# First loads in steps, splits moved to a unit's ends, comparisons in two passes and a last unit in eight products, in a gated expert layer with a diffusion step

## The chip, the cores and the metric

The kernel runs on one core of a Trainium2 chip. The metric is the device time of one execution in microseconds; lower is better. A core has TensorE (PE, matrix products into PSUM, with PEld its weight loads), VectorE (DVE), ScalarE (ACT), GpSimd (POOL) and SyncE (SP, which here issues nearly all DMAs). Each engine works through its own instructions in order and waits on semaphores for the others.

## The reference

`x` is 128 sequences of 64 rows of 256. Each sequence has a type; one of five experts is chosen by it, and two shared dense layers run for all. The three outputs are mixed by softmax weights made from row 0 of each, and added to `x`. Then one explicit diffusion step with reflecting edges and a reaction term is added, with three factors per sequence.

```python
def dense(x, wi, wo): return relu(x @ wi) @ wo          # 256 -> 1024 -> 256
s0, s1 = dense(x, swi[0], swo[0]), dense(x, swi[1], swo[1])
eo = relu(x @ wi[type_label]) @ wo[type_label]
w = softmax(relu(concat(eo[:, 0], s0[:, 0], s1[:, 0]) @ g1) @ g2)
y = x + eo * w[0] + s0 * w[1] + s1 * w[2]
lap_x = y[:, :, left] - 2 * y + y[:, :, right]          # reflecting pads
lap_y = y[:, up, :] - 2 * y + y[:, down, :]
out = y + zX * lap_x + zY * lap_y + zR * y * (1 - y)
```

## The kernel before, in words

**Numbers in two parts.** Every matmul operand is split into a high part that the fast f32 format of PE holds and a rest (`split`: ACT writes the high part, DVE or POOL subtracts). A product of two split operands is three matmuls (high by high, high by low, low by high).

**The shared layers.** The rows are cut into 16 tiles of 4 rows for all 128 sequences (512 columns). Two tiles (a and b, index l) and one shared layer make an *item*: items 0 to 15, item n holding pair n // 2 and layer n % 2. An item is four *units* q of 256 hidden columns. `unit` computes the two tiles by two hidden blocks with seven block products in place of eight, from sums of x blocks (T1 to T4) and of weight blocks (S1 to S4, made by `sum_wi`, split by `split_wi`, kept in DRAM by `keep_wi`, loaded again for later pairs by `load_wi`). Its products run in this order: A11 (seeds bank pa, ACT copies it into pb), S2, A12, S3, S1 (bank pd), A22, S4. DVE forms `c` from pd and the copy u; S4 accumulates on pd and so follows the reading of it by c. After A11, A12, S1 and at the end stand the four *hooks* of a unit, numbered 0 to 3, counted through the item as k = 4q + j; `at(k, ...)` puts background work there. Between the products stand the second-layer products of the unit before (`acc`, lines 662 to 692): *wide* ones with the hidden block's high part (512 columns) and *narrow* ones with its low part (256 columns). `hidden` takes the relu on ACT and the rest on DVE.

**Stages.** Items 0 and 1 come first, and while they run the weights of all eight shared units are prepared (`prepare`, `again`, lines 876 to 890) and the sequences are put in an order by expert (`order_batches`, five steps called as `order`). The very first unit pair has its weights before any sums are ready: `plain_units` (line 616) computes units 0 and 1 of item 0 with eight products. Then come the grouped expert products (`stream`), written to DRAM as `eo_d` in groups of sequences. Items 2 to 15 follow; at item 2 the gate's weights are made (`gate_shared`, `gate_expert` and so on). From item 2 on each tile of y is loaded, gets its expert and shared parts (`start_y`, `sums`, `evacuate`) and is diffused (`diffuse_a`, `diffuse_b`) in two halves of two rows; the halo rows of a tile come from its neighbour (`halo`).

**The start.** `load_behind` and the loop above it (lines 191 to 209) issue the loads of x blocks and weight units on SP; a one-column copy on POOL makes a load wait until the first x block has landed.

**The end.** Item 15 goes through `shared_item`, then `end_rows` (line 743): tile 14's diffusion, then for each row of tile 15 the second-layer products, the evacuation, and `begin_row` and `end_row`, which diffuse row by row and store each.

**Order.** From `in_order(True)` on, the program order written in the code is the order of each engine; in `stream` it is off and a scheduler orders DVE, ACT and POOL. Tiles come from pools with a fixed number of buffers: 6 PSUM banks for most products and 2 for pb (`seeded`), 25 buffers of 4 KB and 16 of 2 KB a partition, 2 for the split weights of a unit. A new tile waits for the readers of the buffer that it takes.

Of the kernel before, what the change touches and what calls it, by code (L numbers as in the profile page):

```python
# [16 lines left out]
P = 128  # L17
B, S, D, F = 128, 64, 256, 1024
NE = 5
# [23 lines left out]
def cond_resid_kernel(ctx: ExitStack, tc: tile.TileContext, xg, xs, xn, itok, z, we, ws, g1, g2, out):  # L43
# [147 lines left out]
    def load_behind(u, c0, c1):  # L191
        if u not in wsr:
            wsr[u] = slot4(f"wsr{u}", F32)
        gps.tensor_copy(wsr[u][:, 0, c0 : c0 + 1], xraw[0, 0, 0][:, 0:1])
        load_ws(u, c0, c1)
# [4 lines left out]
    for l in range(2):  # L200
        for k in range(2):
            if l == 1:
                xraw[0, k, l] = slot2(f"xr0_{k}{l}")
                gps.tensor_copy(xraw[0, k, l][:, 0:1], xraw[0, 0, 0][:, 0:1])
                dma(xraw[0, k, l], xs[l, :, k, :])
    load_behind(0, 256, 512)
    load_behind(1, 0, 512)
    load_behind(2, 0, 512)
    load_behind(3, 0, 512)
# [20 lines left out]
    def order_batches():  # L230
# [72 lines left out]
        ge = [const.tile([1, NU], F32, name=f"ge{i}") for i in range(2)]  # L303
        gt = const.tile([1, NU], F32, name="gt")
        vec.tensor_scalar(ge[0], first, base[0:1, 1:2], None, ALU.is_ge)
        vec.tensor_scalar(ge[1], first, base[0:1, NE : NE + 1], float(NE - 1), ALU.is_lt, ALU.mult)
        for e in range(2, NE):
            vec.tensor_scalar(gt, first, base[0:1, e : e + 1], None, ALU.is_ge)
            vec.tensor_add(ge[0], ge[0], gt)
        yield  # L310
        for e in range(NE + 1, 2 * NE):
            vec.tensor_scalar(gt, first, base[0:1, e : e + 1], None, ALU.is_ge)
            vec.tensor_add(ge[1], ge[1], gt)
# [6 lines left out]
    def clear_spare():  # L320

        zero = pool4.tile([P, ST * D], F32, tag="t4", name="zero")
        vec.memset(zero, 0.0)
        r0, r1 = GROUPS[NRUN][0] * NT, NSLOT * NT
        for r in range(r0, r1, P):
            n = min(P, r1 - r)
            dma(eo_d[r : r + n, :], zero[:n, :])
# [161 lines left out]
    def half_rows(t, half):  # L489
        if t == 0:  # L490
            return (2, 2) if half == 0 else (4, 1)
        return (1 + 2 * half, 2)
# [8 lines left out]
    def diffuse_a(t, half, eng=gps, edge=gps):  # L501
# [6 lines left out]
        act.activation(q[:, :n, :], c, AF.Identity, bias=cz[:, 0:1], scale=cz[:, 1:2])  # L508
        edges(a[:, :n, :], c, edge)
        eng.tensor_tensor(a[:, :n, 1 : D - 1], c[:, :, 0 : D - 2], c[:, :, 2:D], ALU.add)  # L510
# [17 lines left out]

    part, zy = {}, {}

    def end_tile(name):
        return small.tile([P, D], F32, tag="s2", name=name)

    def begin_row(r):

        c = yb[NT - 1][:, r, :]
        a, q, zy[r] = (end_tile(f"end_{n}{r}") for n in "aqz")
        last = r == ST + 1
        act.activation(q, c, AF.Identity, bias=cz[:, 0:1], scale=cz[:, 1:2])
        act.activation(zy[r], c, AF.Copy, scale=zt[:, 1:2])  # L540
        vec.tensor_tensor(a[:, 1 : D - 1], c[:, 0 : D - 2], c[:, 2:D], ALU.add)
        edges(a, c, act)
        vec.tensor_mul(q, q, c)
        if last:
            vec.tensor_add(q, q, part[r])
        vec.scalar_tensor_tensor(q, a, zt[:, 0:1], q, ALU.mult, ALU.add)
        if r == ST:
            part[r + 1] = end_tile("end_p")
            act.activation(part[r + 1], c, AF.Copy, scale=cz[:, 2:3])
        part[r] = q  # L550
        if r <= ST:
            vec.tensor_add(q, q, zy[r - 1])

    def end_row(r, queue):
        if r <= ST:
            vec.tensor_add(part[r], part[r], zy[r + 1])
        queue.dma_start(out[:, ST * (NT - 1) + r - 2, :], part[r])

# [56 lines left out]

    def plain_units():
# [4 lines left out]
        def weights(u):  # L621
            w.append(slot4(f"wi_plain{u}").rearrange("p h c -> p (h c)").rearrange("p (h f c) -> p h f c", h=2, f=2))
            split(w[u][:, 0, :, :], w[u][:, 1, :, :], wsr[u][:, :, 0:256], vec)

        def tile(u, l, bank=psum):
            x = (xop[0, B11], xop[0, B21]) if l == 0 else (x12, xop[0, B22])
            ps = [bank(f"pu{u}{l}{f}") for f in range(2)]
            for k in range(2):
                for j, (wp, xp) in enumerate(((0, 0), (0, 1), (1, 0))):
                    for f in range(2):  # L630
                        mm(
                            ps[f], w[u][:, wp, f, k * P : (k + 1) * P], x[k][:, xp, :], k + j == 0, k == 1 and j == 2
                        )
            return [lambda f=f: hidden((ha, hb)[l], (0, 2 * u + f), ps[f]) for f in range(2)]
# [6 lines left out]
        for i in (T1, T2):  # L641
            sum_x(0, i, vec)
        run(tile(0, 0))
        weights(1)
        for i in (T3, T4):
            sum_x(0, i, vec)
        run(tile(0, 1))
        split_wo(0)
        wide, narrow = tile_a(0, 0)
        run(tile(1, 0))  # L650
        sum_wi(2, gps)
# [5 lines left out]
        keep_wi(2)  # L657
        run(tile(1, 1, seeded))
# [49 lines left out]
    def shared_item(n, before, bg):  # L708

        last, first = n == 2 * NP - 1, n == 0  # L710
        for q in range(NQ):
# [9 lines left out]
            if first and q == 0:  # L721
                plain_units()
            elif not first or q > 1:
                unit(n, q, gaps, hooks)
# [345 lines left out]
```

## Time and profile before

| | us |
|---|---|
| median of 3 runs (1069.48 to 1069.96) | 1069.76 |
| the profiled execution | 1069.37 |
| its span, first to last instruction | 1067.3 |
| PE busy in the span | 1045.0 |
| DVE busy | 740.1 |
| ACT busy | 542.5 |
| POOL busy | 228.0 |

The mean granted clock of PE is 0.995. Times in the profile are us from the first instruction. A line of the order of time has the start, the length, the engine, the kernel's line, the operation, the tile written and the tiles read, the shapes and a count; in brackets stands how long the engine was idle before it and what ended that. L97 and L82 are helper lines that record every DVE, ACT and POOL operation and every matmul, so groups are told apart by their tiles. Lengths of matmuls are modelled and overlap; the distance from start to start is the pace.

### The profile page before, as it was taken

Reading aid. Unit: us, or ns where it says so; the run is one execution under the profiler, and the core shown is the slowest. Engines: PE = TensorE matmul, PEld = TensorE weight load, DVE = VectorE, ACT = ScalarE, POOL = GpSimd, SP = SyncE. Lnnn points to the kernel's source line nnn. Section 1 sums busy time; section 2 is a strip of 40 time slices with the busy share of each in tenths; the row PEclk is TensorE's granted clock in tenths of the full one; section 3 lists DMA queues with packets and bytes.
Section 4 is the critical chain, followed back from the end, with each engine's and each line's share of the span. In section 5 each row is a group of like instructions: output and inputs, shape, how many; then the busy total and the mean of one; then the engine's idle time right before and its main releaser. Section 6 shows DMA issues by size and latency. Waiting matters only on the chain.

```text
span 1067.3 us, 15675 instructions
## 1 busy us (share of the span) xinstructions
PE 1045.0 (98%) x5478; PEld 893.9 (84%) x5478; DVE 740.1 (69%) x1289; ACT 542.5 (51%) x1005; POOL 228.0 (21%) x220
## 2 busy tenths in 40 slices
PE   8999999999999999999999999999999999999995
PEld 6878888888888889988878888888888888888885
DVE  6786745455455556857879778687687687686768
ACT  5565645554455546653446445455355364364353
POOL 3212100100001000221252232242242152052020
PEclk9999999999999999999999999999999999999998
DMA  5347454344443465726335344344253254244221
GB/s 173 124 162 252 151 163 151 119 139 159 159 137 119 139 197 181 244 101 222 109 124 186 124 145 163 104 168 159 73 203 129 69 202 154 80 167 163 105 89 45
DMA packets 65601, 156.12 MB, mean 146 GB/s; under 512 B 7568, under 2 KB 33936, under 8 KB 65520
## 3 DMA queue, kind: packets, MB, share of 16 engines
q1 hardware_dynamic: 62896, 146.18, 40.6%
q0 software_dynamic: 2480, 8.78, 2.3%
q8 instruction: 44, 0.72, 0.3%
q14 instruction: 37, 0.30, 0.1%
q10 hardware_dynamic: 144, 0.13, 0.0%
HBM read 130.16 MB, written 24.90 MB: 145 GB/s over the span
## 4 chain that ended last, share of the span: by engine, by line
PE 53%; DVE 3%; ACT 0%; issue 0%; DVEq 0%
PE acc L82 27%; PE pb L82 11%; PE pd L82 7%; PE pa L82 7%; DVE end_q L97 1%; DVE lq L97 1%; DVE yb L97 0%; DVE x L97 0%; PE pgs L82 0%; DVE end_a L97 0%; DVE pd L97 0%; DVE c L97 0%; DVE lb L97 0%; DVE la L97 0%; ACT pb L97 0%
## 5 line engine op out<-in xcount | busy, mean ns | idle before, releaser
L82 PE MATMUL up<-gxh,gw 128*128 128x512 f32 (+1 forms) x608 | 179.6, 362 | 0.0
L82 PE MATMUL pb<-x,wi 128*128 128x512 f32 x558 | 159.5, 394 | 2.2 <-ACT u L97 1.9
L82 PE MATMUL gacc<-gw,gh 128*128 128x512 f32 (+1 forms) x608 | 141.7, 375 | 0.0
L97 DVE SCALAR_TENSOR_TENSOR gl<-up,gh 128x512 fp32r<-128x512 f32 x112 | 77.0, 688 | 90.1 <-ACT gh L97 90.0
L97 ACT ACTIVATE gh<-up 128x512 fp32r<-128x512 f32 (+1 forms) x152 | 81.8, 539 | 110.4 <-PE up L82 109.5
L97 DVE TENSOR_TENSOR gw<-gwr,gw 128x512 fp32r<-128x512 f32 x152 | 105.4, 722 | 43.9 <-ACT gw L97 43.5
L82 PEld LDWEIGHTS gacc<-gw,gh 128*128 128x128 f32 x608 | 110.0, 188 | 20.9
L82 PEld LDWEIGHTS up<-gxh,gw 128*128 128x128 f32 x608 | 110.5, 189 | 16.5
L97 ACT ACTIVATE u<-pb 128x512 f32<-128x512 f32 x124 | 74.2, 598 | 93.7 <-PE pb L82 89.1
L82 PEld LDWEIGHTS pb<-x,wi 128*128 128x128 f32 x558 | 99.4, 189 | 21.4 <-ACT u L97 3.6
L97 ACT ACTIVATE gw<-gwr 128x512 fp32r<-128x512 f32 x152 | 90.1, 631 | 48.4 <-POOL gxl L97 23.3
L97 POOL TENSOR_TENSOR gxl<-gxr,gxh 128x1024 fp32r<-128x1024 f32 (+1 forms) x19 | 40.1, 2113 | 337.3 <-ACT gxh L97 294.5
L97 DVE SCALAR_TENSOR_TENSOR yb<-acc,wgt,yb 128x256 f32<-128x256 f32 x216 | 99.3, 482 | 18.5 <-PE acc L82 14.8
L82 PE MATMUL up<-gxl,gw 128*128 128x512 f32 (+1 forms) x304 | 110.4, 363 | 0.0
L82 PE MATMUL pd<-x,wi 128*128 128x512 f32 x372 | 106.7, 395 | 3.4 <-DVE c L97 2.6
L82 PE MATMUL pa<-x,wi 128*128 128x512 f32 x372 | 105.1, 391 | 0.9 <-PEq L926 0.9
L97 ACT ACTIVATE pb<-pa 128x512 f32<-128x512 f32 x62 | 36.1, 583 | 119.6 <-PE pa L82 119.4
L82 PEld LDWEIGHTS pd<-x,wi 128*128 128x128 f32 x372 | 69.7, 189 | 21.7 <-DVE c L97 5.5
L82 PEld LDWEIGHTS pa<-x,wi 128*128 128x128 f32 x372 | 68.8, 188 | 14.9 <-issue 1.1
L97 POOL TENSOR_SCALAR la<-yb 128x4 f32<-128x4 f32 (+1 forms) x28 | 9.5, 341 | 280.9 <-ACT yb L97 279.2
L97 DVE TENSOR_TENSOR c<-pd,u 128x512 f32<-128x512 f32 x62 | 42.7, 689 | 32.5 <-PE pd L82 18.0
L82 PEld LDWEIGHTS gacc<-gw,gl 128*128 128x128 f32 x448 | 61.1, 190 | 4.4
(222 smaller groups left out, 2149.2 us busy)
## 6 DMA issues: line engine op xcount, KB each, us to landing
wi<-wi_d SPq DMA_DIRECT2D x56, 896.0 KB, 4.7
gwr<-we_in SPq DMA_DIRECT2D x72, 512.0 KB, 4.6
gxr<-xg_in SPq DMA_DIRECT2D x132, 64.0 KB, 2.6
xr<-xs_in SPq DMA_DIRECT2D x32, 256.0 KB, 5.2
eo_d<-ge SPq DMA_DIRECT2D x64, 128.0 KB, 1.8
yb<-xn_in SPq DMA_DIRECT2D x16, 512.0 KB, 6.0
y_out<-lq SPq DMA_DIRECT2D x29, 256.0 KB, 2.0
wi_d<-wi SPq DMA_DIRECT2D x8, 896.0 KB, 4.4
```

The costliest lines, as they stand in the source:

```text
L82: nc.tensor.matmul(out_ap, lhsT=lhsT, rhs=rhs, start=start, stop=stop, skip_group_check=True)
L97: ins = call(*args, **kwargs)
```

## The change

- **First loads.** `load_behind` becomes `behind` and `load_ws_behind`: a load waits for a named tile. Behind the first x block go the two other x blocks and the first-layer half of unit 1; behind the third x block unit 0's second half and unit 1's; behind the fourth unit 2; behind unit 1's first half unit 3.
- **First units.** T1 and T2 are summed after the first tile's products, T3 and T4 after unit 2's weights; unit 2's weight sums are issued earlier on POOL.
- **Hooks.** In `prepare` the two parts of `split_wi` and `split_wo` move one hook back (k + 2, k + 3, k + 4). `sum_wi(4)` and the sums of `again` go from POOL to DVE. `split_x` of T4 and `split_wo(2)` change hooks.
- **Order.** Eight comparisons, each with an addition, become two comparisons of 35 x 4 and two reductions, in one step instead of two; the steps sit at other hooks. The memset of `clear_spare` goes from DVE to POOL.
- **Gate.** `gate_expert` and `gate_hidden_e` move from hooks 6 and 8 to 4 and 6.
- **Diffusion.** The edge columns follow the sum of neighbours in `diffuse_a`. Tile 0's second half moves from hooks 10, 12, 13, 14 to 14, 16, 17, 17, and `halo(1)` from 13 to 12. Tile 15 is diffused with tile 14's last row in halves of two rows (that row and its own first) and of one row; its last two rows are done apart.
- **Last unit.** Item 15's unit 3 is computed by `end_unit` with eight products from plainly split weights and x, loaded by `load_last` instead of the prepared unit; tile a's part comes first. The last row but one gets its linear part from PE, by products with three diagonal matrices.

```diff
-    load_behind(0, 256, 512)
-    load_behind(1, 0, 512)
-    load_behind(2, 0, 512)
-    load_behind(3, 0, 512)
+    b11 = xraw[0, 0, 0]
+    for k in range(2):
+        xraw[0, k, 1] = slot2(f"xr0_{k}1")
+        behind(b11, xraw[0, k, 1], lambda: dma(xraw[0, k, 1], xs[1, :, k, :]))
+    load_ws_behind(b11, 1, 0, 256)
+    load_ws_behind(xraw[0, 0, 1], 0, 256, 512)
+    load_ws_behind(xraw[0, 0, 1], 1, 256, 512)
+    load_ws_behind(xraw[0, 1, 1], 2, 0, 512)
+    load_ws_behind(wsr[1][:, 0, 0:256], 3, 0, 512)
...
+        cmp = const.tile([1, NU, NE - 1], F32, name="cmp")
+        for i in range(2):
+            b = base[0:1, i * NE + 1 : i * NE + NE]
+            vec.tensor_tensor(
+                cmp, first.unsqueeze(2).to_broadcast([1, NU, NE - 1]), b.unsqueeze(1).to_broadcast([1, NU, NE - 1]),
+                ALU.is_ge,
+            )
+            vec.tensor_reduce(ge[i], cmp, AX.X, ALU.add)
...
-        vec.memset(zero, 0.0)
+        gps.memset(zero, 0.0)
...
             at(k, lambda: sum_wi(u, gps)),
-            at(k + 1, lambda: split_wi(u, (0,))),
-            at(k + 2, lambda: split_wi(u, (1,)), lambda: keep_wi(u)),
-            at(k + 3, lambda: split_wo(u)),
+            at(k + 2, lambda: split_wi(u, (0,))),
+            at(k + 3, lambda: split_wi(u, (1,)), lambda: keep_wi(u)),
+            at(k + 4, lambda: split_wo(u)),
...
-        sum_wi(u, gps)
+        sum_wi(u, vec)
...
-                parts.append(at(6, gate_expert, lambda: load_y(2)))
-                parts.append(at(8, gate_hidden_e, lambda: load_eo(0)))
+                parts.append(at(4, gate_expert))
+                parts.append(at(6, gate_hidden_e, lambda: load_y(2)))
+                parts.append(at(8, lambda: load_eo(0)))
...
-                parts.append(diffusion(0, 7))
-                parts.append(at(13, lambda: halo(1)))
+                parts.append(diffusion(0, 7, True, 7, (0, 1, 1)))
+                parts.append(at(12, lambda: halo(1)))
...
+                parts.append(at(4, lambda: load_last(n)))
+                parts.append(at(8, lambda: split_last_w(n)))
+                parts.append(at(9, lambda: split_last_x(n)))
+                parts.append(at(10, diagonals))
...
+    def plain_tile(n, q, l, w, x, bank, apart=False):
+
+        ps = [bank(f"pu{n}_{q}{l}{f}") for f in range(2)]
+        todo = [(k, j, wp, xp) for k in range(2) for j, (wp, xp) in enumerate(((0, 0), (0, 1), (1, 0)))]
+        order = [(f, *t) for f in range(2) for t in todo] if apart else [(f, *t) for t in todo for f in range(2)]
+        for f, k, j, wp, xp in order:
+            mm(ps[f], w[:, wp, f, k * P : (k + 1) * P], x[k][:, xp, :], k + j == 0, k == 1 and j == 2)
+        return [lambda f=f: hidden((ha, hb)[l], (n, 2 * q + f), ps[f]) for f in range(2)]
...
+    def end_unit(n, gaps, hooks):
+
+        p, t, q = n // 2, NT - 1, NQ - 1
+        y, w = yb[t], last_op["w"]
+        out_a = plain_tile(n, q, 0, w, (xop[p, B11], xop[p, B21]), seeded, True)
+        finish_late()
+        run(out_a)
+        for g in gaps:
+            run(g)
+        for h in hooks:
+            run(h)
+        wide, narrow = tile_a(n, q)
+        run(wide)
+        run(narrow)
         diffuse_a(t - 1, 0, vec, act)
+        run(plain_tile(n, q, 1, w, (last_op["x"], xop[p, B22]), psum, True))
+        for i in range(2):
+            run(row_work(n, 1, i, range(NF - 2), True))
         for step in range(3):
             diffuse_b(t - 1, 0, step)
+        diffuse_a(t - 1, 1, vec, act)
+        halo(t)
+        for i in range(2):
+            run(row_work(n, 1, i, (NF - 2, NF - 1), True))
+            run(row_work(n, 1, i, range(NF), False))
             if i == 0:
                 for step in range(3):
                     diffuse_b(t - 1, 1, step)
+        diffuse_a(t, 0, vec, act)
+        for step in range(3):
+            diffuse_b(t, 0, step)
+        for i in range(2, ST):
+            if i == ST - 1:
+                diffuse_a(t, 1, vec, act)
+                for step in range(3):
+                    diffuse_b(t, 1, step)
+            run(row_work(n, 1, i, range(NF), True))
+            run(row_work(n, 1, i, range(NF), False))
+        r = ST
+        dx, dy, dc = last_op["d"]
+        lin = psum("lin")[:, 0:D]
+        mm(lin, dc, y[:, r, :], True, False)
+        mm(lin[:, 1:D], dx, y[:, r, 0 : D - 1], False, False)
+        mm(lin[:, 0 : D - 1], dx, y[:, r, 1:D], False, False)
+        mm(lin[:, 0 : D : D - 1], dx, y[:, r, 1 : D - 1 : D - 3], False, False)
+        mm(lin, dy, y[:, r - 1, :], False, False)
+        mm(lin, dy, y[:, r + 1, :], False, True)
...
+        vec.scalar_tensor_tensor(q, y[:, r, :], cz[:, 2:3], q, ALU.mult, ALU.add)
+        nc.scalar.dma_start(out[:, S - 1, :], q)
+        vec.scalar_tensor_tensor(sq, y[:, r, :], cz[:, 1:2], y[:, r, :], ALU.mult, ALU.mult)
+        vec.tensor_tensor(sq, lin, sq, ALU.add)
+        nc.sync.dma_start(out[:, S - 2, :], sq)
```

## The prediction

> **What bounds the kernel now.** I read first the busy time of each engine in stretches of the span (columns: stretch, length, busy us of PE, PEld, DVE, ACT and POOL, granted clock, DMA).
>
> ```profile
> 0.00:50.00 50.00, 44.93 (x209) 35.21 (x210) 34.57 (x66) 28.65 (x57) 15.21 (x38) 1.00 0.41 140
> 50.00:100.00 50.00, 47.58 (x238) 39.65 (x237) 39.67 (x102) 27.16 (x56) 10.95 (x13) 0.97 0.58 195
> 100.00:465.00 365.00, 365.00 (x1967) 316.57 (x1966) 213.10 (x372) 195.64 (x390) 43.44 (x22) 1.00 0.49 157
> 465.00:570.00 105.00, 101.19 (x521) 84.62 (x520) 76.35 (x136) 49.09 (x87) 31.61 (x31) 1.00 0.43 150
> 570.00:1040.00 470.00, 469.88 (x2422) 401.85 (x2421) 354.22 (x569) 231.34 (x391) 126.79 (x117) 1.00 0.39 138
> 1040.00:1068.00 28.00, 16.43 (x132) 15.96 (x130) 22.16 (x47) 10.58 (x25) 0.00 (x0) 0.87 0.12 43
> ```
>
> PE is full from 100 to 465 and from 570 to 1040 us; an edit there gives nothing. Time can come only from the first 100 us, from 465 to 570, and from the end, where PE stops 11 us before the kernel. In full stretches one product of 512 columns follows another after 0.227 us and one of 256 after 0.120; below, a hole is what start to start exceeds that. Then I went through the instructions in order of time at each hole.
>
> ```profile
> 11.76 0.63 ACT L97 ACTIVATE wi_plain<-wsr 128x512 fp32r<-128x512 f32 x1 [2.14 <-DMA wsr<-ws_in]
> ...
> 15.99 0.68 DVE L97 TENSOR_TENSOR wo<-wsr,wo 128x512 fp32r<-128x512 f32 x1
> ...
> 28.66 1.14 DVE L97 TENSOR_TENSOR wi<-wsr,wi 128x256 fp32r<-128x256 f32 x2
> 29.72 0.68 DVE L97 TENSOR_TENSOR c<-pd,u 128x512 f32<-128x512 f32 x1
> ...
> 30.45 0.96 PE L82 MATMUL pd<-x,wi 128*128 128x512 f32 x3 [1.06 <-DVE c L97]
> ```
>
> Three holes: PE 11.03 to 12.44 waits for unit 1's weights to land (1.3 us with the slow row behind it), 15.05 to 16.72 for the low part of wo on DVE (1.55), 28.99 to 30.45 for c, which stood behind wo and wi on DVE (1.35).
>
> ```profile
> 76.73 0.91 DVE L97 MEMSET zero<- 128x1024 f32 x1 [0.16 <-issue]
> ...
> 78.71 0.68 DVE L97 TENSOR_TENSOR pd<-pd,u 128x512 f32<-128x512 f32 x1
> ...
> 79.48 0.60 ACT L97 ACTIVATE h_4b<-pd 128x512 fp32r<-128x512 f32 x1 [3.31 <-DVE pd L97]
> ...
> 80.61 1.28 PE L82 MATMUL pb<-x,wi 128*128 128x512 f32 x3 [1.89 <-ACT u L97]
> ```
>
> The order's small comparisons (71.48 to 76.6) and the memset hold DVE; pd is late, so ACT's h_4b and the copy u queued behind it, and PE waits 2.05 us. Then the clock falls:
>
> ```profile
> 81.10:84.50 3.40, 3.40 (x14) 2.92 (x13) 1.37 (x2) 1.09 (x2) 0.00 (x0) 0.50 0.78 271
> ```
>
> 3.4 us at 0.50 is 1.7 us lost. The same comparisons made c late at 73.17 (0.8 us of hole).
>
> ```profile
> 484.43 0.69 DVE L97 SCALAR_TENSOR_TENSOR h_2b<-pd,h_2b 128x512 fp32r<-128x512 f32 x1 [0.66 <-ACT h_2b L97]
> 485.17 1.16 PE L82 MATMUL pge<-gie,g1t 128*128 128x128 f32 x8 [0.88 <-DVE h_2b L97]
> ```
>
> ```profile
> 542.41 0.68 DVE L97 TENSOR_TENSOR c<-pd,u 128x512 f32<-128x512 f32 x1
> ...
> 543.14 0.97 PE L82 MATMUL pd<-x,wi 128*128 128x512 f32 x3 [1.02 <-DVE c L97]
> ```
>
> The gate's product waits for a PSUM bank that h_2b still reads (1.1 us); two holes at 538.4 and 541.7 (0.95 and 1.3) come from DVE work of tile 0's diffusion and x splits. Last, the end:
>
> ```profile
> 1056.15 0.28 PE L82 MATMUL acc<-wo,h_7b 128*128 128x256 f32 x1
> ...
> 1064.07 0.42 DVE L97 TENSOR_TENSOR end_q<-end_q,end_z 128x256 f32<-128x256 f32 x1
> 1064.52 0.37 ACTq L557 DMA_DIRECT2D y_out<-end_q  x1
> ```
>
> From the evacuation of tile 14 at 1044.59 to 1064.49 DVE is never idle for long: the end is DVE's, not PE's.
>
> **The sum.** It starts from the profiled execution, 1069.4 us (span 1067.3 and 2.1 around it); the median is 1069.8. Positions are in the old time.
>
> *First loads, order of the first units: −3.0.* Unit 1's weight half moves ahead of unit 0's second half, behind four x blocks and one weight half: the sixth 256 KB. The DMA queue had finished 1.45 MB by 8.0 us and 1.6 MB by 8.5, so it lands near 8.5 to 9.9, and ACT is free for it at 9.6; PE wants it at 11.03. Hole one goes: −1.3. For hole two the sums T1, T2 move behind the first hidden pair and T3, T4 far back: DVE does h_0a at 9.3, h_1a, unit 1's low part, T1, T2, h_0b, h_1b, then wo, seven instructions of 0.6 to 0.95 (the 0.95 are those beside POOL's sums), so wo ends at 14.3 to 15.0, where PE now comes at 13.75: a hole of 1.0 instead of 1.55, −0.5. At hole three c is put directly behind h_4a, ahead of wo and wi: −1.2. Bounds: all three, −4.2; nothing but a later wsr2 and wsr3, +0.5 (two weight halves in 1 KB pieces; pieces of 1 to 2 KB moved 0.11 to 0.15 MB in half a us, those of 4 KB 0.2).
>
> *Order in two passes, memset on POOL, c ahead of the splits: −4.5.* Sixteen instructions, 1.7 + 2.2 us, become six and two copies. A 1x140 comparison and its reduction aren't in the trace: between 0.16 (the 128x5 reduction) and 0.42 (a 128x256 addition), I take 0.28 as the 128x140 row; 4 x 0.28 and 4 x 0.2 is 1.9 us, and it stands in one unit where c still starts 0.3 us before PE needs it. The memset (0.91) goes to POOL, which is idle there. So 0.8 + 2.05 + 1.7 are saved. If the clock fell all the same, 2.8.
> The Trainium skill (TensorE: Matmul & The Clock Gate, What's actually happening) says that the clock goes down after an idle window of about 3.4 us. The trace shows the fall after 2.05 us of idle, and 3.4 us as its length; by the rule this idle would not be the cause, the 1.7 would stay, and the sum would be 1059.9; the measurement decides.
>
> *Sums of two weight units on DVE, splits at a unit's seed and end: +0.9.* At 44 and 48 us eight 128x128 additions move from POOL to DVE. DVE has no such row: between 0.17 (128x5) and 0.42 (128x256), I take 0.25, so 1.0 for each four. The first four lie in DVE's idle 1.48 before 46.88. The others push the order's middle step (49.41 to 54.99) back by 0.95, and wo, h_0a and c behind it; as wi now comes after c, c gains 0.55 and is 0.4 late on net: PE waits there 0.45. Then sh, wi, h_1b, h_1a, pd and wi's second part follow at 0.3 to 0.6 each, so that part is ready near 61.45 where PE wants it at 60.95: 0.5. Bounds: 0 if the additions take 0.17, +3.0 if both waits grow by an instruction row. In the other units the second part is ready 4.3 to 4.5 us after the S1 product, and wanted at 4.6: covered by 0.1 to 0.3 us.
>
> *Gate four and two hooks sooner: −1.1.* The hidden product takes a bank whose reader, h_2a, is done at 479.25, and PE comes at 480.9. The transposes move to 476.4; eog, issued at 471.83 and 2.8 us to landing, is there by 475.7 at the latest. If not, +0.7.
>
> *Tile 0's second half diffused later: −1.6.* Three 256-wide DVE instructions (0.90, 0.47, 0.47) leave 539 to 543.5, and three POOL ones (0.67, 0.95, 0.74) leave 533 to 535.4, so POOL's x splits end sooner; beside them DVE rows took 1.72 and 1.78 instead of 0.74 and 0.69. Hole two goes (1.2), of hole one I count half (0.5), and 0.1 comes back where the work lands, among evacuations. Bounds −2.2 and +0.4.
>
> *Last unit and end: −1.9.* PE: 24 products instead of 21, +0.7, and a tile of six small ones behind the last row; neither is on the path. Tile a now stands first: its evacuation starts when 24 + 48 of the narrow ones replace the old sequence, 2.1 us earlier (1042.5). Then DVE: four evacuations 1.55, two sums 1.2, a wait of 0.35 for ACT (edges now wait for the sum and sit ahead of the relu), h_6b and h_7b 1.3, and from 1046.9 three diffusion blocks of 512 at 3.4 each, three single evacuations 0.4, one block of 256 at 2.1 and the last evacuation: 1059.5. The last rows: ACT's scaling 0.65, multiply 0.45, two scalar ones 0.5 each, and a scalar one and an addition for the PE-made row 0.9: 1062.6 against 1064.5. PE's linear row: the gate's 128-wide f32 products leave two records of 0.11, so a 256-wide one costs some 0.45, six end near 1060.1 with the last evacuation at 1059.5: hidden by 2 us; uncovered, they would cost 2.6. The splits of the last weights and x (two 0.63 on ACT, two 0.69 on DVE, three small scalings) fit in gaps of 0.6 to 0.9 before c at 1032; else +0.3. Bounds −3.0 and −0.5.
>
> Sum: −3.0 − 4.5 + 0.9 − 1.1 − 1.6 − 1.9 = −11.2, so **1058.2 us**. The two ends of all bounds are 1054.4 and 1070.9.
>
> **The rivals.** *The holes move on (0.22).* DVE does nearly the same work in the first 100 us; what c gains, the next relu or split loses. For: 39.7 of 50 us busy. Against: PE's wants are 0.3 to 1.5 us behind each. Then hole one, the 2.05 and the clock stay won, and the rest of the first part and the diffusion come back: 1058.2 + 1.7 + 0.8 + 1.6 = 1062.3.
> *Operands late in each prepared unit (0.06): slower.* The weights' second part is ready only 0.1 to 0.3 us before use. If a wait of the size at 80.6 with its clock loss (2.05 + 1.7) came in all four units that follow a prepared one, less the 0.9 counted: 1058.2 + 15.0 − 0.9 = 1072.3. It decides for slower only from four such waits on; against it, DVE would have to be over 2 us late each time.
> *The loads come late (0.05).* wsr2 lands after 13 us and holds POOL's sums, wi and PE's first unit: −3.0 turns to +1.5 and the rest holds: 1062.7.
> *The order on the engines isn't the one written (0.02),* nothing moves: 1069.4. Against: the order of the changed instructions on each engine shows each move.
>
> **Numbers.** The forecast has 0.65. A change under 0.2% (2.1 us) can't be told from none. Forecast, moving holes and late loads are faster: 0.92, less 0.02 for a mix of them that reaches the bounds: 0.90; same 0.02; slower 0.08. Range 1054.5 (nearly all best ends) to 1064.0 (past the second and fourth cases).
>
> **What would show it.** Right: no hole of PE ahead of unit 1's products near 11 us, one of about 1.0 ahead of the first acc, no 0.50 clock before the end, two waits of about 0.5 in the second item's first two units, none at pge, at most one hole near 540, and the last issue some 20.1 us behind tile 14's first evacuation. Wrong: waits of PE for wi's lo parts, a wait for eog at the transposes, or an end that waits for lin.

## The result and the profile after

The changed kernel takes 1061.76 us, the median of six runs (1061.31 to 1063.62), against 1070.2 us (1069.48 to 1072.75) for six of the kernel before: a ratio of 0.992, 95% interval 0.9907 to 0.9933, faster by 8.4 us. The profiled execution took 1061.38 us, its span is 1059.6 against 1067.3. The forecast was 1058.2, within 1054.5 to 1064.0.

The busy time of each engine in the same stretches as before (stretch, length, busy us of PE, PEld, DVE, ACT and POOL, granted clock, DMA):

```profile
0.00:50.00 50.00, 47.97 (x219) 37.47 (x220) 37.41 (x83) 30.46 (x59) 11.21 (x31) 1.00 0.45 150
50.00:100.00 50.00, 49.62 (x254) 41.32 (x253) 39.45 (x92) 30.63 (x63) 7.91 (x10) 1.00 0.68 230
100.00:465.00 365.00, 363.82 (x1968) 315.53 (x1967) 210.47 (x368) 194.60 (x388) 46.07 (x26) 1.00 0.48 152
465.00:570.00 105.00, 104.13 (x528) 86.89 (x528) 83.87 (x144) 50.83 (x89) 34.75 (x32) 1.00 0.48 163
570.00:1040.00 470.00, 469.56 (x2431) 401.52 (x2430) 353.92 (x570) 229.64 (x392) 120.73 (x111) 1.00 0.38 134
1040.00:1068.00 28.00, 13.66 (x102) 12.51 (x100) 15.50 (x29) 3.73 (x9) 0.00 (x0) 0.94 0.12 42
```

PE does 3 us more in the first 50 us than before (47.97 against 44.93), 2 us more in the next 50, and the granted clock there is 1.00 instead of 0.97. From 465 to 570 it does 2.9 us more, of which 1.1 only moved: the wait at the start of item 2 now lies ahead of 465. DVE's 15.50 us from 1040 on, against 22.16, are no shorter end, since tile 14's evacuation now begins ahead of 1040: from there to the last issue DVE is busy for 19.1 us in both profiles.

Positions of the same PE instruction in both profiles say where each microsecond went. The shift is its start after minus its start before; the change in a stretch is the difference to the row above, and minus is a gain.

| mark on PE | start before | shift | change in the stretch | forecast |
|---|---|---|---|---|
| first product of item 1 | 47.52 | −2.61 | −2.61 | −3.0 |
| unit (1,2) | 66.31 | −1.49 | +1.12 | +0.9 |
| first grouped product | 99.89 | −5.82 | −4.33 | −4.5 |
| item 2 | 466.43 | −5.82 | 0 | 0 |
| behind the gate | 492.38 | −6.89 | −1.07 | −1.1 |
| item 4 | 552.29 | −7.63 | −0.74 | −1.6 |
| item 15 | 1008.42 | −6.31 | +1.32 | 0 |
| last DMA issue | 1064.52 | −8.02 | −1.71 | −1.9 |
| end of the span | 1067.27 | −7.67 | +0.35 | 0 |

The instructions of the changed kernel in order of time (start, busy us, engine, line, operation, out<-in; in brackets the idle time before and what ended it) at the places that the prediction spoke of. First the order's comparisons:

```profile
68.89 0.29 DVE L97 TENSOR_TENSOR cmp<-io,base 1x140 f32<-1x140 f32 x1
...
69.21 0.29 DVE L97 TENSOR_REDUCE ge<-cmp 1x35 f32<-1x140 f32 x1
...
70.68 0.67 DVE L97 TENSOR_TENSOR c<-pd,u 128x512 f32<-128x512 f32 x1
...
73.35 0.69 DVE L97 TENSOR_TENSOR pd<-pd,u 128x512 f32<-128x512 f32 x1
...
74.42 0.85 PE L82 MATMUL pb<-x,wi 128*128 128x512 f32 x3
```

The 1x140 comparison and its reduction, which the trace of before did not have, take 0.29 each, at a pitch of 0.2 to 0.3; c follows at 70.68, pd at 73.35, and the product pb at 74.42 waits for nothing. The 2.05 us hole and the 3.4 us at half clock are gone.

Where PE still waits, early:

```profile
20.40 0.95 DVE L97 TENSOR_TENSOR xt<-xr,xt 128x512 f32<-128x512 f32 x1
...
21.27 0.68 DVE L97 SCALAR_TENSOR_TENSOR h_2b<-pu,h_2b 128x512 fp32r<-128x512 f32 x1
...
22.04 0.58 ACT L97 ACTIVATE pb<-pa 128x512 f32<-128x512 f32 x1 [0.90 <-DVE h_2b L97]
...
22.67 0.96 PE L82 MATMUL pb<-x,wi 128*128 128x512 f32 x3 [0.52 <-ACT pb L97]
```

pb waits for ACT's copy, the copy for h_2b on DVE, and h_2b stands behind the sums T3 and T4, which take 0.95 each beside POOL's sums of unit 2's weights. Those start 2 us later than before (15.18 against 12.99; 13.6 to 14.7 in the other profiles with the new loads), since unit 2's weights land later. This hole (0.7 us) wasn't in the forecast; the one ahead of the first acc, forecast at 1.0, is 0.23 here.

In item 1's first units:

```profile
54.55 0.67 DVE L97 TENSOR_TENSOR c<-pd,u 128x512 f32<-128x512 f32 x1
...
55.27 0.98 PE L82 MATMUL pd<-x,wi 128*128 128x512 f32 x3
...
57.55 0.68 DVE L97 TENSOR_TENSOR pd<-pd,u 128x512 f32<-128x512 f32 x1
...
58.15 0.67 DVE L97 TENSOR_TENSOR wi<-wsum,wi 128x512 fp32r<-128x512 f32 x1
...
58.87 0.50 PE L82 MATMUL pb<-x,wi 128*128 128x512 f32 x1 [0.32 <-DVE wi L97]
```

The two waits in item 1's first units are there: pd at 55.27 follows c, and the third pb at 58.87 follows wi's second part, which DVE takes at 58.15, directly behind pd.

Where tile 0 is diffused:

```profile
526.58 1.78 DVE L97 SCALAR_TENSOR_TENSOR h_5b<-c,h_5b 128x512 fp32r<-128x512 f32 x1
...
527.77 3.00 POOL L97 TENSOR_TENSOR x<-xr,x 128x512 fp32r<-128x512 f32 x2
...
529.48 1.83 DVE L97 SCALAR_TENSOR_TENSOR lq<-lb,zt,lq 128x512 f32<-128x512 f32 x1
...
531.23 1.09 DVE L97 TENSOR_TENSOR x<-xt,x 128x512 fp32r<-128x512 f32 x1
...
531.77 0.96 PE L82 MATMUL pb<-x,wi 128*128 128x512 f32 x3 [0.49 <-ACT u L97]
...
532.25 0.68 DVE L97 SCALAR_TENSOR_TENSOR h_4b<-pd,h_4b 128x512 fp32r<-128x512 f32 x1
...
532.98 0.97 PE L82 MATMUL pd<-x,wi 128*128 128x512 f32 x3 [0.25 <-DVE h_4b L97]
```

Here two holes were to become none or a half. They stand at 531.77 (0.65) and 532.98 (0.41): DVE's h_5b and lq take 1.78 and 1.83 us instead of 0.7, h_5b beside POOL's last sum of x (526.06, 1.74), lq beside its splits of x (two in 3.00), and u, then h_4b, are late by that.

And the last of the end:

```profile
1052.87 0.48 DVE L97 SCALAR_TENSOR_TENSOR yb<-acc,wgt,yb 128x256 f32<-128x256 f32 x1
...
1053.40 0.70 PE L82 MATMUL lin<-yb,diag 128*128 128x256 f32 x2 [0.29 <-DVE yb L97]
...
1056.05 0.42 DVE L97 TENSOR_TENSOR end_s<-lin,end_s 128x256 f32<-128x256 f32 x1
1056.50 0.33 SPq L802 DMA_DIRECT2D y_out<-end_s  x1
```

The end is DVE's, as forecast. PE's last two products of lin start at 1053.40, 0.05 us behind DVE's last evacuation, and end at 1054.1; the addition that reads lin comes at 1056.05. lin is hidden by two microseconds. From tile 14's first evacuation, at 1036.17, to the last issue are 20.33 us; the forecast had 20.1.

### The profile page after: what moved, and what is told of

It reads as the page before. It is cut to its first block, busy times and chain, and to the rows that moved or that the text cites. A ratio compares the mean times of both kernels' runs of the same rounds, so it can differ in the third digit from the quotient of the medians.

```text
span 1059.6 us, 15690 instructions
## 1 busy us (share of the span) xinstructions
PE 1048.8 (99%) x5493; PEld 895.2 (84%) x5493; DVE 740.6 (70%) x1282; ACT 539.9 (51%) x996; POOL 220.7 (21%) x210
## 4 chain that ended last, share of the span: by engine, by line
PE 50%; DVE 5%; issue 1%; ACT 1%; DVEq 0%
PE acc L82 27%; PE pb L82 10%; PE pd L82 7%; PE pa L82 6%; DVE lq L97 2%; PE pu L82 1%; DVE pd L97 0%; DVE c L97 0%; DVE h_3a L97 0%; DVE h_5b L97 0%; DVE yb L97 0%; ACT h_3a L97 0%; PE pgs L82 0%; DVE la L97 0%; DVE end_q L97 0%
## 5 line engine op out<-in xcount | busy, mean ns | idle before, releaser
L82 PE MATMUL pd<-x,wi 128*128 128x512 f32 x366 | 104.5, 394 | 0.8 <-DVE h_4b L97 0.2
L97 POOL TENSOR_TENSOR la<-yb 128x508 f32<-128x508 f32 (+1 forms) x28 | 31.8, 1134 | 281.5 <-ACT yb L97 280.0
```

What stands on the lines that cost most here:

```text
L82: nc.tensor.matmul(out_ap, lhsT=lhsT, rhs=rhs, start=start, stop=stop, skip_group_check=True)
L97: ins = call(*args, **kwargs)
```

## The experiments

All are the changed kernel with an edit, except the first two. Times are medians of four to six runs, that of the kernel before once more is a single one. The kernel before ran beside each on the same chip: 1070.8 us beside the changed kernel's second run and the two edits after it and the old order, 1069.3 to 1069.7 beside the others. Where tenths matter, the shifts of the marks above are compared and not the medians.

### The kernel before, and the changed kernel, once more

> The kernel before, unchanged, profiled a second time. It tells the chip's own spread from what the change did. Theory A: the holes of PE at 11, 15, 29, 73, 78 to 80, 482, 538 and 541 us are set by the order of the instructions and come back within 0.3 us of their sizes; the 0.50 clock after the hole at 78 to 80 hangs on where the throttle's window stands and may be missing (then the span is some 1.7 us shorter, 1065.6), and the moment at which the clock first rises may lie anywhere from 4.8 to 10.2 us. Theory B: the small holes of 0.3 to 0.4 us that the changed kernel shows between 565 and 945 us came with the change: here there is none of them (PE was busy 469.88 of 470 us in the first profile). Rival: they turn up here too, one to five of them, and the loss of 1.0 to 1.3 us across those items is the chip's and not the change's.

Measured: 1070.1 us, span 1068.0. The holes come back at the same places within 0.1 us. So does the half clock:

```profile
77.90:81.40 3.50, 1.62 (x8) 1.03 (x7) 3.08 (x6) 1.57 (x3) 0.00 (x0) 1.00 0.69 199
81.40:84.80 3.40, 3.40 (x14) 3.01 (x13) 1.39 (x3) 1.23 (x2) 0.00 (x0) 0.50 0.82 275
```

Three small holes of some 0.3 us stand at 701, 784 and 872 us, of which the first profile had the middle one. In order of time at the first:

```profile
698.61 1.75 POOL L97 TENSOR_TENSOR xt<-xr,xt 128x512 f32<-128x512 f32 x1
...
699.73 1.18 DVE L97 SCALAR_TENSOR_TENSOR lq<-lb,zt,lq 128x512 f32<-128x512 f32 x1
...
700.83 0.68 DVE L97 TENSOR_TENSOR c<-pd,u 128x512 f32<-128x512 f32 x1
...
701.56 0.73 PE L82 MATMUL pd<-x,wi 128*128 128x512 f32 x2
```

lq, beside POOL's sum xt, takes 1.18 us instead of 0.7; c is late by the difference and PE's pd at 701.56 is 0.3 us late. Across items 4 to 14 this execution loses 0.61 us against the other one of the same kernel. So part of the +1.32 of the table can come without the change.

> The changed kernel once more, for a second profile of it. In its first profile PE lost 1.3 us in items 4 to 13 (new holes near 569, 694 and 943 us) that the kernel before did not lose. Theory (the new order of the edge columns on POOL makes them): they stand at the same three places, within 0.2 us each. Rival (chance: which DVE and POOL instructions meet differs from one execution to the next): they stand elsewhere or are missing. The clock's rise near 7.1 us (6.0 in the profile of before) should move by up to 1 us if it is chance.

Measured: 1061.23 us, ratio 0.9913 (0.990 to 0.9926). The shifts are those of the table within 0.7 us; items 4 to 14 lose 1.26. One thing differs: the hole ahead of the first acc is 1.12 us, as forecast, and the one at 22 us is away. In this execution the clock rose at 4.8 us, in the first profile at 7.1. Where the clock rises 2.3 us later, PE's last product ahead of the acc starts 0.77 us later, DVE's wo does not (13.79 and 13.91), and the mark of unit (0,2) is nearly the same: −2.19 there, −2.07 here.

### Edges ahead of the sum again

```diff
-        eng.tensor_tensor(a[:, :n, 1 : D - 1], ...)
-        edges(a[:, :n, :], c, edge)
+        if eng is gps: edges(...)
+        eng.tensor_tensor(a[:, :n, 1 : D - 1], ...)
+        if eng is not gps: edges(...)
```

> Only the order of the edge columns on POOL is undone (edges ahead of the sum of neighbours, as before). Theory that this order makes the holes of items 4 to 13: PE's way from the start of item 4 to the start of item 15 is 1.0 to 1.5 us shorter than in the changed kernel, time 1060.4. Rival, chance: within 0.3 us of the changed kernel, with holes at other places.

Measured: 1060.92 us, 0.9906 (0.9892 to 0.992). Items 4 to 14 lose 0.99, with holes at 615, 693, 859 and 943 us. Of the late holes the edges' place makes one: the hole near 569 us, in item 4, went, the rest stayed. It stands in all eleven profiles with the new order on POOL, where the shift across it changes by +0.34 to +0.40 us, and in none of the three with the old.

### T3 and T4 behind the second pair of unit 1

```diff
-        for i in (T3, T4):
-            sum_x(0, i, vec)
         run(tile(1, 1, seeded))
+        for i in (T3, T4):
+            sum_x(0, i, vec)
```

> The sums T3 and T4 go behind the last plain products of unit 1, so behind h_2b and h_3b on DVE. Theory (the 0.8 us hole of PE ahead of unit 2's S2 product near 22 us is h_2b standing behind T3 and T4, which run beside POOL's weight sums at 0.95 instead of 0.69): the hole goes, PE is 0.6 to 0.8 us earlier from there on, time 1061.1. Rival (T3's split is then late for the S3 product, or T4 for A22): the hole moves 2 to 4 us on, and the time stays within 0.2 us.

Measured: 1061.87 us, 0.9919 (0.9906 to 0.9932). The rival holds, as the order of time shows:

```profile
20.14 0.69 DVE L97 SCALAR_TENSOR_TENSOR h_2b<-pu,h_2b 128x512 fp32r<-128x512 f32 x1 [0.66 <-ACT h_2b L97]
...
21.34 0.68 DVE L97 TENSOR_TENSOR xt<-xr,xr 128x512 f32<-128x512 f32 x1
...
22.06 0.63 ACT L97 ACTIVATE x<-xt 128x512 fp32r<-128x512 f32 x1 [1.47 <-DVE xt L97]
...
22.60 0.58 ACT L97 ACTIVATE pb<-pa 128x512 f32<-128x512 f32 x1
...
23.23 0.50 PE L82 MATMUL pb<-x,wi 128*128 128x512 f32 x1 [0.74 <-ACT pb L97]
```

h_2b is now early (20.14), but on ACT the split x<-xt stands ahead of the copy pb and waits for T3. The hole moved from one queue to the other and grew from 0.7 to 0.9.

### The order as before

```diff
-        for i in range(2): one comparison of 1x140, one reduction
-        gps.memset(zero, 0.0)
+        vec.tensor_scalar and vec.tensor_add for each expert, in two steps
+        vec.memset(zero, 0.0)
```

> The order's comparisons one by one in two steps at hooks 9 and 10 and the memset of the spare rows on DVE, as before; all else as changed. Theory (the comparisons and the memset made the 2.05 us hole and the fall of the clock): the hole near 75 us and 3.4 us at half clock come back, 3.0 to 4.5 us lost, time 1065. Rival (what helped was that c now stands ahead of the splits and that wo moved back): the hole stays under 1 us, the clock stays up, loss under 1.0 us, time under 1062.5.

Measured: 1066.65 us, 0.9952 (0.994 to 0.9964). From unit (1,2) to the first grouped product the shift changes by −0.90 instead of −4.33. In order of time:

```profile
76.31 0.91 DVE L97 MEMSET zero<- 128x1024 f32 x1 [0.16 <-issue]
...
78.89 0.67 DVE L97 TENSOR_TENSOR wi<-wsum,wi 128x512 fp32r<-128x512 f32 x1
...
79.61 0.50 PE L82 MATMUL pb<-x,wi 128*128 128x512 f32 x1 [2.82 <-DVE wi L97]
```

The busy times from 78.5 us on (columns as above):

```profile
78.50:81.90 3.40, 2.29 (x10) 1.90 (x11) 2.77 (x5) 2.32 (x4) 0.00 (x0) 1.00 1.02 316
```

The memset and the comparisons, at their old hooks, make the hole: 2.98 us ahead of the pb at 79.61, whose wi part DVE starts only at 78.89. The clock stayed at 1.00 all the same. So in this kernel, where the splits stand later, this part's price is 3.4 us by waits alone; a fall of the clock, 1.7 us in both profiles of the kernel before, would come on top. The median is 4.9 to 5.4 us above the changed kernel's two. Of the 5.95 us by which the profiled span is longer than the changed kernel's first one, 3.4 lie here, 1.4 ahead of unit (1,2), where the clock rose only at 10.2 us, and 0.9 in items 4 to 14.

### The loads as before

```diff
-    load_ws_behind(b11, 1, 0, 256)
-    load_ws_behind(xraw[0, 0, 1], 0, 256, 512)
-    load_ws_behind(xraw[0, 0, 1], 1, 256, 512)
+    load_ws_behind(xraw[0, 0, 0], 0, 256, 512)
+    load_ws_behind(xraw[0, 0, 0], 1, 0, 512)
```

> The changed kernel with the loads' chain of before: every first load waits for the first x block alone, unit 1's weights behind both halves of unit 0's. Theory: hole one comes back near 11 us (1.3 us ahead of unit 1's products), but unit 2's weights land near 13 instead of 15 us, so POOL's sums start 2 us sooner, T3 and T4 on DVE do not run beside them at 0.95 each, and the hole of 0.8 to 0.9 at 22 us goes: 1.3 - 0.85 = +0.5, 1061.7 against the changed kernel's 1061.2. Rival, the loads bring what I put down for them and the hole at 22 us is not theirs: +1.3, 1062.5. Rival two, all of the 2.65 us that the start gained is the loads': 1063.9. The clock's first rise moves single profiles by up to 2 us, so positions are compared from the first unit's end on.

Measured: 1062.95 us, 0.9933 (0.992 to 0.9947). Not one hole comes back but two (in order of time):

```profile
11.89 0.63 ACT L97 ACTIVATE wi_plain<-wsr 128x512 fp32r<-128x512 f32 x1 [2.23 <-DMA wsr<-ws_in]
...
12.55 0.69 DVE L97 TENSOR_TENSOR wi_plain<-wsr,wi_plain 128x512 fp32r<-128x512 f32 x1 [1.94 <-ACT wi_plain L97]
...
12.57 3.01 PE L82 MATMUL pu<-x,wi_plain 128*128 128x512 f32 x12 [1.51 <-ACT wi_plain L97]
...
16.12 0.68 DVE L97 TENSOR_TENSOR wo<-wsr,wo 128x512 fp32r<-128x512 f32 x1
...
16.85 0.50 PE L82 MATMUL acc<-wo,h_0a 128*128 128x512 f32 x1 [1.27 <-DVE wo L97]
```

ACT waits for unit 1's weights until 11.89, DVE's part of them until 12.55 and PE until 12.57 (1.68 us). On DVE the sums T1 and T2, h_0b, h_1b and then wo stand behind that part, so wo slips to 16.12 and the first acc to 16.85 as it was before (1.43 us of hole). The hole at 22 us is gone, as the theory had it, and T3 and T4 take 0.68 each. But PE also comes over 2 us later to this place, so the run doesn't show that the loads alone made that hole. On net the first grouped product is 4.36 us earlier than before instead of 5.8 to 6.4: the loads' chain is worth 1.5 to 2.1 us, and the place of c directly behind h_4a, which stands in this kernel too, the 1.2 us at 30.

### The two units' sums on POOL

```diff
-        sum_wi(u, vec)
+        sum_wi(u, gps)
-        at(16, lambda: sum_wi(4, vec), ...
+        at(16, lambda: sum_wi(4, gps), ...
```

> The changed kernel with the sums of the two weight units (unit 4's and the repeated ones of units 0 and 1) on POOL again, as before. Theory: on DVE they cost the 1.35 us of loss that the two profiles show between 24 and 67 us (eight additions of 0.28, waits of 0.3 at 47, 0.34 at 55 and 0.59 at 58): without them those waits go or shrink to under 0.2 each and the time is 1060.0 to 1060.5. Rival: the sums cost nothing by themselves; the waits at 55 and 58 come from the later splits (one hook further back), stay at 0.3 and 0.6, and the time is 1061.2 within 0.4. Rival two, the sums on POOL come late for wi (POOL takes 0.46 to 0.9 each): a wait of over 0.5 us near 47 and near 99 us, 1062.

Measured: 1061.49 us, 0.9925 (0.9912 to 0.9939). The wait at 55 us goes, that at 58 stays (0.47), and a new one of 0.97 stands at 31.24, ahead of a third pb that waits for wi's second part. Nothing is gained.

### Splits at the old hooks, alone and with the sums

```diff
-            at(k + 2, lambda: split_wi(u, (0,))),
-            at(k + 3, lambda: split_wi(u, (1,)), lambda: keep_wi(u)),
-            at(k + 4, lambda: split_wo(u)),
+            at(k + 1, lambda: split_wi(u, (0,))),
+            at(k + 2, lambda: split_wi(u, (1,)), lambda: keep_wi(u)),
+            at(k + 3, lambda: split_wo(u)),
```

> The changed kernel with the splits of a prepared unit's weights at the old hooks (one, two and three behind the sums instead of two, three and four). Theory: the waits of 0.3 at 54 to 56 and of 0.5 to 0.9 at 58 us are theirs, since the second part of wi now stands behind pd on DVE, and go: from the mark at unit (0,3)'s first product to unit (1,2)'s the loss falls from 1.2 to 0.3 us, the time to 1060.5. Rival: as in the kernel before, c then stands behind wi and wo on DVE, and holes of 0.7 to 1.2 us come back at 28 and at 71 us: 1062.0 to 1063.0.

Measured: 1060.88 us, 0.9918 (0.9904 to 0.9932). The wait at 58 us goes, but two of 0.35 stand at 54 and 55, behind the middle step of the order that the sums on DVE push back.

> Both of the parts for which I put down a loss undone: splits at the old hooks and the sums of the two units on POOL. Theory: each brings what it brings alone, and nothing else happens: the splits' 0.9 and the sums' 0.0 to 0.3, 1060.3 to 1060.6. Rival: the two are one part, in that the sums went to DVE because POOL's come late for splits at the old hooks: waits of 0.5 us and more at 28 to 31, 45 to 47 and 97 to 99 us, 1062 or above.

Measured: 1060.07 us (1059.33 to 1061.56), 0.9915 (0.9901 to 0.9929). With both, item 1's waits are gone altogether (busy times from 50 to 100 us):

```profile
50.00:100.00 50.00, 50.00 (x260) 42.42 (x259) 39.67 (x83) 32.41 (x66) 11.25 (x14) 1.00 0.66 224
```

In order of time, where the second wait was:

```profile
54.81 0.67 DVE L97 TENSOR_TENSOR wi<-wsum,wi 128x512 fp32r<-128x512 f32 x1
...
56.91 0.84 PE L82 MATMUL pb<-x,wi 128*128 128x512 f32 x3
```

PE is busy for all of the 50 us, pb at 56.91 follows wi's second part of 54.81 by more than a microsecond. From item 1's start to unit (1,2) the shift changes by −0.02 here, by +1.12 in the changed kernel, by +1.03 with the old splits alone, and with the sums on POOL alone by +1.58 (counted from unit (0,3), where its new wait lies). The first grouped product is 7.70 us earlier than before, 1.3 to 1.9 more than in the changed kernel. By the medians it is the fastest of all, 1.2 to 1.7 us below the changed kernel, but by ratio (0.9915 against 0.992 and 0.9913) the gain isn't shown.

### Tile 0's second half where it was

```diff
-                parts.append(diffusion(0, 7, True, 7, (0, 1, 1)))
-                parts.append(at(12, lambda: halo(1)))
+                parts.append(diffusion(0, 7))
+                parts.append(at(13, lambda: halo(1)))
```

> The changed kernel with the diffusion of tile 0's second half at its old hooks (three DVE and three POOL instructions back among the units near 531 to 536 us). Theory, from the traces: the move gained 0.76 us, because only the second hole (1.2 us) shrank to 0.5 and the first one stayed: +0.8, 1062.0. Rival, my forecast's price: two holes of 0.95 and 1.3 come back whole, +1.6, 1062.8. Rival two: the hole of 0.66 at 531 belongs to POOL's splits of x, which stand there either way, and the move gained nothing: 1061.2.

Measured: 1062.05 us, 0.9928 (0.9915 to 0.9942). The holes are 0.86 and 1.17 again, and from the gate to item 4 the shift changes by +0.02 instead of −0.74. The move is worth 0.7 us.

### Gate and end as before

```diff
-                parts.append(at(4, gate_expert))
-                parts.append(at(6, gate_hidden_e, lambda: load_y(2)))
+                parts.append(at(6, gate_expert, lambda: load_y(2)))
+                parts.append(at(8, gate_hidden_e, lambda: load_eo(0)))
...
-            elif last and q == NQ - 1:
-                end_unit(n, gaps, hooks)
+            end_rows(n)
```

> The changed kernel with two parts undone that stand 550 us apart and are read at their own places: the gate's expert part at its old hooks, and the last unit and the end rows as before (seven products, tile a last, no linear row on PE, edges ahead of the sum). Theory, from the two traces: PE waits 1.1 us ahead of pge again near 477 us, so item 3 starts 1.1 later against the changed kernel; and the last issue moves from 8.0 to 8.6 us below before's to 1.7 to 1.9 later again, the kernel's end by 1.4 to 1.9. Sum +2.5 to +3.0: 1063.7 to 1064.2. Rival for the gate: eog or the bank is not what PE waited for, and the hole stays away: 0. Rival for the end: what the changed end gains is only the 2.11 us by which tile 14's evacuation is earlier, and 0.4 of it is lost behind it, so that from tile 14's first evacuation to the last issue the old rows take 19.9 and the new ones 20.3.

Measured: 1063.99 us, 0.9945 (0.9931 to 0.9959). With the old end the edges go ahead of the sum again on DVE, not on POOL. At the gate, in order of time:

```profile
478.46 0.69 DVE L97 SCALAR_TENSOR_TENSOR h_2b<-pd,h_2b 128x512 fp32r<-128x512 f32 x1 [0.66 <-ACT h_2b L97]
...
479.20 0.82 PE L82 MATMUL pge<-gie,g1t 128*128 128x128 f32 x5 [0.85 <-DVE h_2b L97]
```

pge waits for h_2b again and the shift changes by +0.03 across the gate instead of −1.07. From item 15 to the last issue the shift does not change at all (−5.41, −5.40), where the changed kernel gains 1.71. The old rows take 19.94 us from tile 14's first evacuation (1039.18) to the last issue (1059.12), the new ones 20.33: the end gains because that evacuation is 2.1 us earlier, and gives 0.4 of it back. So at the end the rival holds, and the theory's 1.7 to 1.9 come out of it.

### wo ahead of the second hidden pair

```diff
+        split_wo(0)
         run(tile(0, 1))
-        split_wo(0)
```

This edit is made on the kernel with both splits and sums undone.

> The changed kernel with the old hooks of the splits, the two units' sums on POOL, and one edit more: the split of unit 0's wo stands ahead of the second hidden pair of unit 0 instead of behind it, so that on DVE it passes h_0b and h_1b. Theory: in the kernel with the first two edits PE waits 1.12 us ahead of its first acc product, for wo's low part, which DVE starts at 14.16 behind h_0b and h_1b (0.60 apart each); 1.2 us sooner, the hole falls to under 0.2 us and everything behind it comes 0.9 to 1.1 sooner: 1059.0 to 1059.4 against 1060.07, provided the clock rises as early (4.4 us). Rival: the second half of unit 0's weights lands only just before ACT takes it at 11.95; then ACT waits for it with h_0b and h_1b queued behind, and the hole stays at 0.5 us or more: 1059.6 to 1060.2. Rival two: the hole moves to the hole of 0.4 to 0.9 that some runs show at 22 us, ahead of pb, where h_2b on DVE and the copy pb on ACT end late: the first unit gains 1.0, the second unit gives 0.5 of it back.

Measured: 1060.43 us (1059.53 to 1061.03), 0.9911 (0.9894 to 0.9927). The hole ahead of the first acc is gone and the first unit ends 2.37 us earlier than before, against 1.78 without the edit, though in this execution the clock rose at 7.2 us instead of 4.4. But a wait of 0.54 us is back at 54 us. The medians lie within each other's ranges; whether it helps isn't decided.

## Why the prediction held, and where it was off

*The order* (−4.5, measured −4.33): right, step by step. The 1x140 row taken at 0.28 is 0.29. Undone, it costs 3.4 us by a wait of 2.98, without a fall of the clock in that execution: the 1.7 of the clock is seen in both profiles of the kernel before and is not certain in every one.

*First loads and first units* (−3.0, measured −2.61). Holes one and three went as forecast. Hole two was not a matter of DVE's order alone, as I had it: with the old loads it stays whole, so the loads bring 1.5 to 2.1 of the 2.6 to 3.2 us on net. The hole left ahead of the first acc, forecast at 1.0, measures from under 0.25 to 1.15 us, and the clock's rise alone doesn't set it (0.23 with a rise at 7.1 us and with one at 5.1). The unforeseen 0.7 at 22 us stands behind T3 and T4, which POOL's sums of unit 2's later weights slow to 0.95; I had later weights only in the bound. Whether the hole opens also hangs on when PE comes: in the second profile of the changed kernel T3 and T4 take the same 0.95, PE waits 1.12 ahead of the acc, and no hole follows.

*Sums and late splits* (+0.9, measured +1.12): size and places right, 55 and 58 us. My working followed both waits down one queue and gave them one price; my expectation for undoing both added the parts one by one. By the marks, undoing either one gains little or nothing and undoing both gains 1.1 to 1.3 us.

*Gate* (−1.1, measured −1.07): right, and its hole comes back when undone.

*Diffusion* (−1.6, measured −0.74, and 0.7 by undoing it): right in kind, too large. The step that failed is the 1.2 for hole two and half of hole one. The two together went from 2.03 to 1.07 us, and 0.2 came back where the work lands. POOL's last sum of x and its splits still meet DVE's h_5b and lq there, each stretched to 1.8 us, so u and h_4b stay late.

*Items 4 to 14* (0, measured +1.32): the sentence that PE is full from 570 to 1040 us, so that nothing there moves, failed. It was read from one execution. The second profile of before loses 0.61 there, the twelve profiles that carry the change, whole or with an edit, lose 0.75 to 2.2. The busy share doesn't show it (469.56 of 470 us here); the starts of one instruction in two profiles do. The holes stand at a few fixed places, and which of them open differs by execution. In the table's +1.32 are 0.38 for the hole in item 4, which the edges' order makes, twice 0.56 for holes in items 7 and 13, and −0.2 elsewhere.

The larger ones have one place in each of items 7, 9, 11 and 13, where DVE's lq and POOL's second sum of x meet. In item 7, the changed kernel first, then the kernel before:

```profile
688.62 1.29 POOL L97 TENSOR_TENSOR xt<-xr,xt 128x512 f32<-128x512 f32 x1
688.72 1.74 DVE L97 TENSOR_TENSOR lq<-lq,yb 128x512 f32<-128x512 f32 x1
```

```profile
695.89 0.68 DVE L97 TENSOR_TENSOR lq<-lq,yb 128x512 f32<-128x512 f32 x1
...
696.08 1.65 POOL L97 TENSOR_TENSOR xt<-xr,xt 128x512 f32<-128x512 f32 x1
```

The one that starts first keeps its length, the other is stretched. All fourteen profiles at these four places go by that order: 39 times POOL's sum starts 0.02 to 0.11 us ahead of lq, lq takes 1.73 to 1.82 us, and the hole of about 0.3 at the pd behind c stands; 17 times it starts with lq or later, and there is no hole. POOL's sums wait for the load of x, so a tenth of a microsecond in its landing decides. Kernels with the change have this hole in 36 of 48 cases, the kernel before in 3 of 8; why their loads come that much sooner beside DVE's work was not tried and stays open, as do smaller shifts of 0.1 to 0.4 us at two other places.

*The end* (−1.9, measured −1.71): right, with lin hidden by 2 us as worked out. From the last issue to the end of the span are 3.10 us instead of 2.75. The last issue is on SP's queue now and was on ACT's. With the old end rows on ACT's queue it is 3.17 in one profile, with SP's queue and the old loads 2.68 in another, so the queue alone doesn't set it; the cause is open.

Of the 3.5 us by which the forecast of the span was too low, 1.3 are items 4 to 14, 0.9 the diffusion, 0.4 the start, 0.35 the tail, and 0.2 each the late splits, the order and the end. The time is nearer to that of the rival in which the holes move on (1062.3) than to the forecast, but by another way: that rival gave back c's 0.8 near 73 us and hole three, and both stayed won. The rival of late operands came true in the two waits that the forecast counted and no further. The loads came late only for POOL's sums. The order on the engines was the one written. Of the signs named, two failed in the first profile: ahead of the first acc stands 0.23 us, not about 1.0, and near 540 us two holes, not at most one. The wait for wi's second part at 58 us, a kind of wait listed as a sign of being wrong, is the one that the sum had counted. Two slips in the working are small: by its own pace of 0.227 us holes two and three and the two of tile 0 were 1.44, 1.23, 0.86 and 1.18 us, 0.1 less each than written, and the worst ends of the bounds add up to 1070.7, not 1070.9.

## What to carry to other kernels

A stretch that one profile shows as full is full in that execution; a second profile of the kernel before would have shown the holes, and that the forecast's zero there had an uncertainty of a microsecond. Where a load's landing decides which of two engines goes first, one such meeting was worth half a microsecond here, in some executions and not in others. Two edits that feed one queue (here DVE, through the sums and the splits) are to be priced together and undone together. Where a hole is removed, ask what its cause stands behind one step further back: wo was late through h_0b and h_1b, and these through a load.

## What the runs showed of the hardware

*The clock goes by windows.* The changes of the granted clock lie whole multiples of 3.413 us apart: from 6.0 to 81.1 us 22 of them, from 7.1 to 1058.4 in the changed kernel 308. Where the first rise falls differs by execution: between 4.3 and 7.3 us in thirteen profiles, at 10.2 in one. Idle of 2.05 and 2.04 us inside one such window (77.7 to 81.1, and 78.0 to 81.4) brought the clock down for the next one. Idle of 2.98 us did not: it lay across a boundary at 78.43, 1.80 us before and 1.18 behind it. What share of a window has to be idle doesn't come out: by the records PE is busy for 1.77 us of the window up to 78.43, and the clock stayed, while at the end of the kernel with the edges ahead of the sum it is busy for 1.86 us of a window, and the clock fell behind it. The Trainium skill (TensorE: Matmul & The Clock Gate, What's actually happening) says that the window is free-running and 3413 ns long, which these runs agree with; that a whole idle window is needed they contradict.

*DVE beside POOL.* A DVE instruction with two SBUF inputs that takes 0.7 us alone took 1.18, 1.78 and 1.83 beside POOL's. The Trainium skill (SBUF — State Buffer, SBUF: two separate sides) describes a port pair that the one that starts first holds for its whole instruction while the other waits; the two pairs of rows of item 7 agree, with 1.29 of POOL and then 1.74 of DVE, and with 0.68 of DVE and then 1.65 of POOL. Three kinds of wait that the change left go back to such pairs: T3 and T4 at 22 us, h_5b and lq at 530, and lq ahead of c in the late items.
